# Two layers of outlook attention: softmax, shift matmuls, bands and contractions of layer 1 one to two columns later, with five input buffers and three band buffers

## The chip, the core and the metric

The kernel runs on one core of a Trainium2 chip. A core has five engines with instruction streams of their own: TensorE (matmuls and transposes), VectorE, ScalarE, GpSimd and SyncE, and 16 DMA engines that move data between the device memory and the core's SBUF. TensorE writes to PSUM. The metric is the device time of one execution in microseconds. A profiled execution gives the trace that is read here; in its pages PE is TensorE, PEld the weight loads of TensorE, DVE VectorE, ACT ScalarE, POOL GpSimd and SP SyncE.

## What is computed

The input x has 8 images of 56 x 56 positions and 384 channels, in float32. Two layers are applied one after the other, each with a group normalisation (32 groups) ahead of it and a residual around it:

```python
x = x + layer0(gn(x))    # 12 heads, attention of 9 x 9 logits per position and head, folded back
x = x + layer1(gn(x))    # 6 heads, attention of 9 logits per position and head
```

The change is in layer 1:

```python
a  = x_map @ W_attn + b_attn                            # 9 logits per head and position
a  = softmax(a.reshape(B, H * W, heads, 9), axis=-1)
v  = x_map @ W_v + b_v
vp = pad(v, 1)                                          # patches: the 3 x 3 neighbourhood
y  = einsum('bpKhd,bphK->bphd', patches, a)             # 9 neighbours, weighted
y  = y @ W_proj + b_proj
```

So each position takes logits and values from a projection, a softmax over nine neighbours, a weighted sum over the 3 x 3 neighbourhood of v for each of six heads of 64 channels, and an output projection.

## The kernel before

**Two stages.** Layer 0 runs first and lasts to about 2356 us of the span; layer 1 follows. TensorE's instructions are held in program order (lines 119 and 122). The other engines' instructions are ordered by a scheduler, which may move an instruction ahead of others whose inputs come later.

**Groups and steps of layer 1.** Images are worked on in four pairs, and the 56 columns of a pair in eight groups of PX = 7 columns: 32 groups, of 7 x 112 positions (two images of 56 rows). The loop (line 932) takes one step per column, written as (g, m), group and column in the group. For its main part it is a software pipeline: while the logits and values of group g are made, group g-1 goes through softmax, contraction and output projection.

**The chain of a group.**

- `load` (line 718) brings the group's input, transposed, from memory into a buffer x1t, on SyncE's queue. There are four buffers: three in the pool io1, and one (each fourth group) in the pool late0 of layer 0.
- `normed` (line 728, instructions at line 740) is the group normalisation on ScalarE, from x1t to xn, in two parts of three and four columns.
- `attend` (line 769) takes 128 positions: six matmuls, 2.2 us, to 54 logits and 384 values. VectorE adds the biases (lines 779 and 782), and ScalarE issues stores of v to a table in memory (line 296). Eight columns are seven tiles of 128 positions, so the attend of every eighth column is left out.
- `regroup` (line 789) stores the logits of a group to memory (line 796, ScalarE's queue, written lgtab) and reads them back with the image row across the partitions (line 804, SyncE's queue, written at).
- `weigh` (line 813) is the softmax: maximum and difference on VectorE (818, 819), Exp on ScalarE (820), sum and reciprocal on VectorE (822, 823), and the multiplication on GpSimd (824).
- `move` (line 826): 0/1 matmuls with shifted identities (pw) bring a row's weights to its neighbours; ScalarE copies them into a diagonal layout wz (845), which is stored to a table ztab (847, ScalarE's queue).
- `fetch` (line 855) loads the value patches vp (361) and the bands z (308), both on SyncE's queue, and appends 14 jobs. Four of them are contractions: for each of two images, tiles 0 to 3 in two pairs. Tile b_t makes pc in PSUM by up to 12 small matmuls of z and vp each, and ScalarE copies pc to yT (883). There are two PSUM buffers for pc (NC = 2). Between the contractions lie the last transposes of the group before, and six further jobs are the output projection (po, 899) with the first three transposes (pt, copied at 912, and stored at 914).

**Who sets the order.** Jobs are taken in order of their appending, two per step (`jobs.run`), once due. Before the change the loop calls weigh(g-1) in the step of m = 2, and move(g-1) and fetch(g-1) in that of m = 3, with the jobs due four steps later. So TensorE's order through a group is: pw of the group, then projections of the group before, with attends and transposes between, then the contractions, at the columns m = 0 to 3 of the next group.

**The band buffers.** Layer 0 has two band tiles `zs`; layer 1 uses the halves of these as four band buffers, so that the two images of a group alternate between pairs.

Of the kernel before, what the change touches and what calls it, by code (L numbers as in the profile page):

```python
# [15 lines left out]
def two_outlook_layers(  # L16
# [32 lines left out]
    nc = tc.nc  # L49
# [3 lines left out]
    NCH = C // P  # L53
    IMG = 2
    R = IMG * H
    MARGIN = 2
# [8 lines left out]
    PX = 7  # L65
    NPX = W // PX
    T = IMG * H * PX
# [14 lines left out]
    PY0, NPY0, SX0, SY0 = 7, 8, PX + 4, 11  # L82
    ROW0 = HEADS0 * PX
    WT = 2 * SX0 - E0
    PY1, NPY1, SX1, SY1 = 8, 7, PX + 2, 10
    ROW1 = HEADS1 * PX
# [217 lines left out]
    def bands(queue, z, table, line, slot, row, top, groups, b, py, npy):  # L304

        for (s0, s1), (m0, m1) in groups:
            first = (b * H + top) * line + s0 * slot + m0 * row
            queue.dma_start(
                z[s0:s1, :, m0 * row : m1 * row],
                bass.AP(  # L310
                    table.tensor, table.offset + first + bands.at[row],
                    [[slot, s1 - s0], [py * line, npy], [1, (m1 - m0) * row]],
                ),
            )
# [65 lines left out]
    def layer0(late, pools):  # L380
# [14 lines left out]
        def stats_chunk(pair, blk, i, alone):  # L395

            nm = f"{pair}_{blk}"
            if blk == 0 and i == 0:
                stats[pair] = stat.tile([P, NCH, IMG, NBLK, 6], F32, tag="st0", name=f"st0_{pair}")
            if i == 0:  # L400
                xts[pair, blk] = io.tile([P, NCH, XB, R], F32, tag="xt", name=f"xt_{nm}")
            xr, xt = xrs[pair, blk], xts[pair, blk]
            if alone:
                pt = bank(P, 0, XB * R).rearrange("p (m r) -> p m r", m=XB)
            else:
                pt = ps.tile([P, XB, R], F32, tag="t", name=f"pt_{nm}_{i}")
            for j in range(XB):
                transpose(pt[:, j, :], xr[:, j, i * P : (i + 1) * P], ident[:R, :R])
            nc.scalar.copy(xt[:, i], pt)
            for b in range(IMG):  # L410
                nc.vector.bn_stats(stats[pair][:, i, b, blk, :], xt[:, i, :, b * H : (b + 1) * H])
            if i == NCH - 1:
                nc.sync.dma_start(
                    xTs[pair][:, :, blk * XB * R : (blk + 1) * XB * R], xt.rearrange("p i m r -> p i (m r)")
                )
                del xrs[pair, blk], xts[pair, blk]

        stats_load(0, 0, nc.sync)
# [292 lines left out]
    def layer1(pools, base, last_of_layer0, late_w):  # L711
# [3 lines left out]

        x1ts, lgs = {}, {}

        def load(g):
            pair, px = divmod(g, NPX)

            if g % 4 == 3:
                t = late_w.tile([P, NCH, T], F32, tag="xres", name=f"x1t_{g}")
            else:
                t = io.tile([P, NCH, T], F32, tag="x1t", name=f"x1t_{g}", bufs=3)
            nc.sync.dma_start(t, x1s[pair][px])
            x1ts[g] = t.rearrange("p i (m r) -> p i m r", m=PX)

        def normed(g, m0, m1):
# [28 lines left out]

        NW = SX1 * K * ROW1
        wzs = [fixed.tile([R, NW + PX + 1], F32, name=f"wz1_{n}") for n in range(2)]

        NZ = 4
        half_z = NPY1 * PY1 * ROW1
        zs1 = [
            zs[n // 2].rearrange("p n e -> p (n e)")[: SX1 * SY1, n % 2 * half_z : (n % 2 + 1) * half_z]
            .rearrange("p (n e) -> p n e", n=NPY1)
            for n in range(NZ)
        ]

        def attend(g, m):

# [55 lines left out]
        def move(g):  # L826
# [25 lines left out]
                wz[:, :NW].rearrange("r (s e) -> r s e", s=SX1),  # L852
            )

        def fetch(g, due):
            pair, px = divmod(g, NPX)
            n_tile = 2
            yT = projected(f"1_{g}")
            x1t = x1ts.pop(g)
            vps = [patch_tiles(f"1_{g}", b)[: SX1 * SY1, :NPY1] for b in range(IMG)]  # L860
            for b in range(IMG):
                rows_to_patches(vps[b], vtab1, px, b * H + MARGIN - 1, PY1, NPY1, SX1)
            for b in range(IMG):
                z, vp = zs1[(g * IMG + b) % NZ], vps[b]
                bands(
                    nc.sync, z, ztab1[g % NTAB], LINE1, SLOT1, ROW1, MARGIN - 1, GROUPS1,
                    b, PY1, NPY1,
                )

                def contract(t, b=b, z=z, vp=vp):  # L870
                    lo, hi = t * n_tile, min(NPY1, (t + 1) * n_tile)
                    pc = ps.tile([P, NCH, n_tile, PY1, PX], F32, tag="c", name=f"pc1_{g}_{b}_{t}", bufs=NC)
                    for py in range(lo, hi):
                        zp = z[:, py].rearrange("s (y h m) -> s y h m", y=PY1, h=HEADS1)
                        for h in range(HEADS1):
                            i, j = divmod(h, P // D1)
                            matmul(
                                pc[j * D1 : (j + 1) * D1, i, py - lo],
                                vp[:, py, h * D1 : (h + 1) * D1],
                                zp[:, :, h, :],  # L880
                                start=True, stop=True,
                            )
                    nc.scalar.copy(
                        yT[:, :, :, b, lo * PY1 : hi * PY1],
                        pc[:, :, : hi - lo].rearrange("p i n y m -> p i m (n y)"),
                    )

                for t in range(0, (NPY1 + n_tile - 1) // n_tile, NC):
                    jobs.add(due, lambda t=t, f=contract: [f(t + n) for n in range(NC)])

                    jobs.add(due, turning.pop(0) if turning else lambda: None)

            def project_out(half, j):
                lo, hi = HALVES[half]
                n = (hi - lo) * R
                po = ps.tile([P, 4 * R], F32, tag="of"[(half * NCH + j) % 2], name=f"po1_{g}_{half}_{j}")
                project_half(po, wo_t, yT, half, j)
                res = x1t[:, j, lo:hi].rearrange("p m r -> p (m r)")
                nc.vector.scalar_tensor_tensor(  # L899
                    res, po[:, :n], bo_t[:, j : j + 1], res, ALU.add, ALU.add  # L900
                )

            def turn(m):

                half = m // 4
                lo, hi = HALVES[half]
                if m == lo:
                    fetch.ot = io.tile([R, 4, C], F32, tag="ot", name=f"ot_{g}_{half}")
                pt = banks[-1][:R, :C] if m % 2 else ps.tile([R, C], F32, tag="t", name=f"pt1_{g}_{m}")
                for i in range(NCH):  # L910
                    transpose(pt[:, i * P : (i + 1) * P], x1t[:, i, m, :], ident)
                nc.scalar.copy(fetch.ot[:, m - lo, :], pt)
                if m == hi - 1:
                    nc.sync.dma_start(
                        of[pair * R : (pair + 1) * R, px * PX + lo : px * PX + hi, :],
                        fetch.ot[:, : hi - lo],
                    )

            out, back = project_out, turn
            for work_of in (  # L920
                (lambda: out(0, 0),), (lambda: out(0, 1),), (lambda: out(0, 2),),
                (lambda: out(1, 0), lambda: back(0)), (lambda: out(1, 1), lambda: back(1)),
                (lambda: out(1, 2), lambda: back(2)),
            ):
                jobs.add(due, lambda work_of=work_of: [w() for w in work_of])
            for m in range(3, PX):
                turning.append(lambda m=m: back(m))
# [1 line left out]
        turning = []  # L929
        NG = NPAIR * NPX  # L930
        stage(0)
        for step in range(NG * PX + 4):
            g, m = divmod(step, PX)
            jobs.run(base + step, 1)
            if step == 0:
                last_of_layer0(base + step + 5)
            if step == 4:
                for wz in wzs:
                    nc.gpsimd.memset(wz, 0.0)
            if g < NG:  # L940
                attend(g, m)
            if g and m == 0:
                regroup(g - 1)
                stage(g)
            if m == 4 and g + 1 < NG:
                load(g + 1)
            if m == 6 and g + 1 < NG:
                normed(g + 1, 0, 3)
            if m == 0 and 0 < g < NG:
                normed(g, 3, PX)  # L950
            jobs.run(base + step, 1)

            if g and m == 2:
                weigh(g - 1)
            if g and m == 3:
                move(g - 1)
                while not clear_bands.done:
                    jobs.run(None, 1)
                fetch(g - 1, base + step + 4)
        jobs.run(None, -1)  # L960
        for w in turning:
# [45 lines left out]
```

## Time and profile before

| | |
|---|---|
| time, median of three | 3598.7 us (3592.17 to 3605.03) |
| span of the profiled execution | 3610.8 us, granted TensorE clock 0.978 |
| TensorE busy | 3460.6 us, 96%, 29078 instructions |
| VectorE, ScalarE, GpSimd busy | 1914.9, 1165.1, 986.4 us |
| layer 0 | 0 to about 2356 us |
| layer 1 | about 2356 us to the end, 32 groups; 36.4 to 37.4 us each |
| moved by DMA | 840.73 MB, 233 GB/s on average |

The columns of the views are told where they are shown. In the views of groups and of the timeline, a line such as "L883 ACT COPY yT<-pc" names the line of the kernel, the engine, the operation, and output and input by the program's names. In brackets at the end of a timeline line stands the engine's idle time just before, with what ended it. Instructions that issue a DMA are marked SPq or ACTq; they take a place in the queue of their engine and the transfer itself goes on elsewhere.

The chain that ended last gives TensorE 78% of the span and DMA 16%. The DMA part holds the bands' way to memory and back (5% and 3%), and the logits' (2% and 1%).

### The profile page before, as it was taken

To read this page: it belongs to the slowest core of one execution; us is meant where nothing else is said; L and a number is where in the kernel's file an instruction comes from. 1 tells how busy PE (TensorE), PEld (TensorE's weight loads), DVE (VectorE), ACT (ScalarE), POOL (GpSimd) and SP (SyncE) were. 2 spreads that over 40 slices of the span, in tenths; PEclk is the share of its full clock that TensorE was granted. 3 is DMA by queue.
4 is the path that set the end of the run, shared out by engine and by line. 5 is a ranking of instruction groups with operands and counts; after the bars stand their busy time and mean duration, and the time that the engine had idled before them with its cause. 6 is when DMAs were issued, how large, how long until landed. Compare 5 with 4: busy or idle time off the path is not lost.

```text
span 3610.8 us, 72232 instructions
## 1 busy us (share of the span) xinstructions
PE 3460.6 (96%) x29078; PEld 2375.8 (66%) x29078; DVE 1914.9 (53%) x4648; ACT 1165.1 (32%) x2727; POOL 986.4 (27%) x1409
## 2 busy tenths in 40 slices
PE   4999999999999999999999999989999999999998
PEld 4667767777777777777767777655565565556555
DVE  3766666667666676667666666532222222222222
ACT  2333322332333333333222322232333433333332
POOL 2444334434444434443444444410000000000000
PEclk6999999999999999999999999999999999999999
DMA  9799988688886778887667777677778787777876
GB/s 294 202 285 292 267 265 257 226 249 263 267 271 208 263 238 254 261 258 262 204 208 241 218 223 231 222 252 188 207 200 220 206 226 196 199 218 198 219 196 159
DMA packets 692253, 840.73 MB, mean 233 GB/s; under 512 B 302222, under 2 KB 596174, under 8 KB 687822
## 3 DMA queue, kind: packets, MB, share of 16 engines
q1 hardware_dynamic: 329614, 576.00, 51.1%
q10 hardware_dynamic: 362304, 260.11, 27.5%
q8 instruction: 229, 3.75, 0.5%
q14 instruction: 106, 0.87, 0.1%
HBM read 514.32 MB, written 321.66 MB: 232 GB/s over the span
## 4 chain that ended last, share of the span: by engine, by line
PE 78%; DMA 16%; DVE 2%; ACT 1%; issue 1%; POOL 1%; ACTq 0%; SPq 0%; POOLq 0%; DVEq 0%
PE bank L119 44%; PE po L119 15%; PE pc L119 11%; DMA ztab<-wz 5%; PE pw L119 4%; DMA z<-ztab 3%; DMA lgtab<-lgt 2%; PE pt L122 2%; DMA at<-lgtab 1%; DMA xr<-in_x 1%; PE bank L122 1%; DMA vtab<-v 1%; DMA x1t<-x 1%; DMA xT<-xt 1%; DMA vp<-vtab 1%
## 5 line engine op out<-in xcount | busy, mean ns | idle before, releaser
L119 PE MATMUL bank<-wa_t,xn 128*112 128x288 f32 x4032 | 1083.6, 408 | 2.2 <-ACT xn L471 2.2
L119 PEld LDWEIGHTS bank<-wa_t,xn 128*112 128x112 f32 x4032 | 691.9, 177 | 253.1 <-issue 31.9
L510 POOL TENSOR_TENSOR at<-at,den 112x972 f32<-112x972 f32 x224 | 504.9, 2254 | 1226.6 <-DVE den L509 1181.7
L119 PE MATMUL po<-yT,wo_t 128*128 128x448 f32 (+1 forms) x2304 | 823.7, 497 | 5.4 <-DVE x1t L621 4.8
L119 PEld LDWEIGHTS po<-yT,wo_t 128*128 128x128 f32 x2304 | 435.3, 192 | 296.2 <-issue 192.2
L119 PE MATMUL pc<-z,vp 121*32 121x49 f32 (+1 forms) x17664 | 490.0, 255 | 50.6 <-DMA z<-ztab 23.1
L119 PEld LDWEIGHTS pc<-z,vp 121*32 121x32 f32 (+1 forms) x17664 | 444.2, 131 | 127.5 <-issue 91.8
L119 PE MATMUL bank<-wc_t,xn 128*128 128x438 f32 x1176 | 485.7, 549 | 3.8 <-DMA wc_t<-in_wv 2.6
L486 DVE TENSOR_REDUCE mx<-bank 112x36 f32<-112x324 f32 x672 | 327.1, 487 | 299.5 <-PE bank L119 292.9
L119 PE MATMUL bank<-wv_t,xn 128*128 128x384 f32 x1176 | 418.6, 492 | 0.0
L824 POOL TENSOR_TENSOR at<-at,den 112x378 f32<-112x378 f32 x32 | 30.2, 945 | 1142.4 <-DVE den L823 704.8
L487 DVE TENSOR_TENSOR at<-bank,mx 112x324 f32<-112x324 f32 x672 | 328.5, 489 | 21.1 <-DVE mx L486 0.5
L491 ACT ACTIVATE at<-at 112x972 f32<-112x972 f32 x224 | 227.1, 1014 | 331.7 <-DVE at L487 307.9
L119 PEld LDWEIGHTS bank<-wc_t,xn 128*128 128x128 f32 x1176 | 216.3, 193 | 177.9 <-issue 167.2
L740 ACT ACTIVATE xn<-x1t,bias,scale 128x168 f32<-128x168 f32 (+4 forms) x498 | 213.6, 503 | 322.1 <-DMA x1t<-x 227.9
L119 PEld LDWEIGHTS bank<-wv_t,xn 128*128 128x128 f32 x1176 | 219.5, 191 | 139.5 <-issue 18.6
L899 DVE SCALAR_TENSOR_TENSOR x1t<-po,bo_t,x1t 128x448 f32<-128x448 f32 (+1 forms) x192 | 120.1, 626 | 339.6 <-PE po L119 339.6
L555 ACT COPY wt<-pw 112x120 f32<-112x120 f32 x224 | 58.0, 259 | 662.1 <-PE pw L119 577.5
L533 POOL TENSOR_TENSOR pre<-at,at 112x108 f32<-112x108 f32 (+1 forms) x440 | 238.0, 541 | 115.0 <-DVE wt L556 100.6
L779 DVE TENSOR_TENSOR lgt<-bank,ba_t 128x54 f32<-128x54 f32 x196 | 41.1, 210 | 417.2 <-PE bank L119 417.1
L503 DVE TENSOR_TENSOR d<-at 112x432 f32<-112x432 f32 x224 | 141.1, 630 | 196.9 <-ACT at L491 196.9
L600 ACT COPY yT<-pc 128x294 f32<-128x294 f32 x256 | 103.3, 408 | 372.1 <-PE pc L119 318.8
(81 smaller groups left out, 2845.4 us busy)
## 6 DMA issues: line engine op xcount, KB each, us to landing
z<-ztab SPq DMA_DIRECT2D x64, 2352.0 KB
vp<-vtab SPq DMA_DIRECT2D x64, 1536.0 KB
ztab<-wt ACTq DMA_DIRECT2D x336, 183.8 KB
vp<-vtab SPq DMA_DIRECT2D x64, 945.0 KB
xT<-xt SPq DMA_DIRECT2D x56, 672.0 KB
xin<-xT ACTq DMA_DIRECT2D x56, 672.0 KB
xres<-xT SPq DMA_DIRECT2D x32, 1176.0 KB
x1t<-x SPq DMA_DIRECT2D x32, 1176.0 KB
```

Source lines behind the costliest of these rows:

```text
L119: tc.keep_in_program_order(nc.tensor.matmul(*args, **kwargs))
L122: tc.keep_in_program_order(nc.tensor.transpose(*args, **kwargs))
L486: nc.vector.tensor_reduce(mx[:, pi, :], pl.rearrange("r q a -> r a q"), AX.X, ALU.max)
L487: nc.vector.tensor_tensor(at[:, pi], pl, mx[:, pi, :].unsqueeze(1).to_broadcast([R, K2, PH]), ALU.subtract)
L491: nc.scalar.activation(at, at, AF.Exp, scale=SCALE0)
L503: nc.vector.tensor_add(d4, at[:, :, 0:4], at[:, :, 4:8])
L510: nc.gpsimd.tensor_tensor(at, at, den.unsqueeze(2).to_broadcast([R, K, K2, PH]), ALU.mult)
L533: nc.gpsimd.tensor_tensor(dst, terms[0], terms[1], ALU.add)
L555: nc.scalar.copy(mid[:, 0 : E0 : E0 - 1, :], pw[:, 0 : E0 : E0 - 1, :])
L600: nc.scalar.copy(yT[:, :, :, b, rows_of], pc.rearrange("p i n y m -> p i m (n y)"))
L740: nc.scalar.activation(to[:, i, :, rows], x1ts[g][:, i, lo - first : hi - first, rows], AF.Identity, bias=bias[:, i, b : b + 1], scale=sca ...
L899: nc.vector.scalar_tensor_tensor(res, po[:, :n], bo_t[:, j : j + 1], res, ALU.add, ALU.add)
```

## The change

Softmax, shift matmuls, bands and contractions of a group are each placed later in the loop, so that the waits between them have more time. The input load goes one column earlier. As a group then stays open for longer, a fifth input buffer is taken, out of the fourth half of the band tiles, and the band buffers go from four to three. The band loads get a function of their own, called right behind the shift matmuls, and the loop runs two steps longer. The store of a transposed input in the opening part of layer 0 is held in program order.

| step of a group in the loop | before | after |
|---|---|---|
| load of the next input | m = 4 | m = 3 |
| weigh | m = 2 | m = 3 |
| move | m = 3 | m = 4 |
| band loads | m = 3, behind vp | m = 4 |
| vp loads, jobs appended | m = 3 | m = 5 |
| contractions run at the next group's | m = 0 to 3 | m = 2 to 5 |

```diff
@@ stats_chunk (layer 0)
-                nc.sync.dma_start(
+                store = nc.sync.dma_start(
                     xTs[pair][:, :, blk * XB * R : (blk + 1) * XB * R], xt.rearrange("p i m r -> p i (m r)")
                 )
+                if alone:
+                    tc.keep_in_program_order(store)
@@ layer1
+        NZ = 3
+        half = NPY0 * PY0 * ROW0 // 2
+        halves = [z.rearrange("p n e -> p (n e)")[:, n * half : (n + 1) * half] for z in zs for n in range(2)]
...
-            if g % 4 == 3:
+            if g % 5 == 3:
                 t = late_w.tile([P, NCH, T], F32, tag="xres", name=f"x1t_{g}")
+            elif g % 5 == 4:
+                t = halves[3][:, : NCH * T].rearrange("p (i t) -> p i t", i=NCH)
             else:
                 t = io.tile([P, NCH, T], F32, tag="x1t", name=f"x1t_{g}", bufs=3)
...
-        NZ = 4
-        half_z = NPY1 * PY1 * ROW1
-        zs1 = [
...
+        zs1 = [t[: SX1 * SY1, : NPY1 * PY1 * ROW1].rearrange("p (n e) -> p n e", n=NPY1) for t in halves[:NZ]]
...
+        def fetch_bands(g):
+            for b in range(IMG):
+                bands(
+                    nc.sync, zs1[(g * IMG + b) % NZ], ztab1[g % NTAB], LINE1, SLOT1, ROW1, MARGIN - 1,
+                    GROUPS1, b, PY1, NPY1,
+                )
...
-        for step in range(NG * PX + 4):
+        for step in range(NG * PX + 6):
...
-            if m == 4 and g + 1 < NG:
+            if m == 3 and g + 1 < NG:
                 load(g + 1)
...
-            if g and m == 2:
+            if g and m == 3:
                 weigh(g - 1)
-            if g and m == 3:
+            if g and m == 4:
                 move(g - 1)
                 while not clear_bands.done:
                     jobs.run(None, 1)
+                fetch_bands(g - 1)
+            if g and m == 5:
                 fetch(g - 1, base + step + 4)
```

More of the change, by code (lines that the diff above doesn't have):

```diff
@@ L716, in layer1 @@
         x1ts, lgs = {}, {}
+        NZ = 3
+        half = NPY0 * PY0 * ROW0 // 2
+        halves = [z.rearrange("p n e -> p (n e)")[:, n * half : (n + 1) * half] for z in zs for n in range(2)]
+        assert half >= NPY1 * PY1 * ROW1 and half >= NCH * T
         def load(g):
             pair, px = divmod(g, NPX)
-            if g % 4 == 3:
+            if g % 5 == 3:
                 t = late_w.tile([P, NCH, T], F32, tag="xres", name=f"x1t_{g}")
+            elif g % 5 == 4:
+                t = halves[3][:, : NCH * T].rearrange("p (i t) -> p i t", i=NCH)
             else:
@@ L759, in layer1 @@
         wzs = [fixed.tile([R, NW + PX + 1], F32, name=f"wz1_{n}") for n in range(2)]
-        NZ = 4
-        half_z = NPY1 * PY1 * ROW1
-        zs1 = [
[L764 to L767, printed above, removed]
+        zs1 = [t[: SX1 * SY1, : NPY1 * PY1 * ROW1].rearrange("p (n e) -> p n e", n=NPY1) for t in halves[:NZ]]
         def attend(g, m):
@@ L864, in fetch @@
                 z, vp = zs1[(g * IMG + b) % NZ], vps[b]
[L865 to L868, printed above, removed]
                 def contract(t, b=b, z=z, vp=vp):
```

## The prediction

> **What bounds the kernel now.** I read the page's shares first: TensorE is busy 3460.6 of 3610.8 us (96%). Then a table of windows, to see in which layer the other 4% lie. Its columns are the window, its length, busy time and count of TensorE, its weight loads, VectorE, ScalarE and GpSimd, the granted clock, the DMA share and GB/s.
>
> ```profile
> 1000.00:1100.00 100.00, 100.00 (x1103) 72.38 (x1102) 68.00 (x172) 34.22 (x70) 40.20 (x56) 1.00 0.77 234
> 2800.00:2900.00 100.00, 95.06 (x772) 59.55 (x771) 28.36 (x62) 39.76 (x123) 2.84 (x3) 1.00 0.80 208
> 3000.00:3100.00 100.00, 93.82 (x600) 57.30 (x601) 26.07 (x56) 35.45 (x109) 2.23 (x3) 0.95 0.82 212
> ```
>
> Layer 0 (up to about 2356) leaves TensorE no gap; layer 1 leaves 4 to 6 us in 100. Layer 1 is 1255 us with 1173.5 busy: 81.5 us idle. So the change can win at most about 82 us and the clock loss that goes with it; other engines have room. The waits of TensorE in 2500 to 3550 (28 groups of seven columns, 54 of 1050 us idle) name the causes (total, times, longest):
>
> ```profile
> PE pw L119 <- POOL at L824: 19.1, 13, 3.7
> PE pc L119 <- DMA z<-ztab: 18.6, 11, 3.1
> PE pc L119 <- issue: 10.3, 5, 3.3
> PE pc L119 <- ACT yT L883: 4.3, 7, 0.8
> ```
>
> The 0/1 matmuls pw wait for the softmax's last multiplication, the contractions pc for their bands z. Both are the same chain, logits to memory and back, softmax, pw, bands to memory and back, contractions, reaching TensorE a little late. That is what the change loosens.
>
> A short gap costs twice:
>
> ```profile
> 3439.65 2.82 PE L119 MATMUL pc<-z,vp 90*64 90x56 f32 x48 [3.29 <-issue]
> ```
>
> 48 contraction matmuls after 3.29 us of idling take 2.82 us; elsewhere 1.61.
>
> [...] gaps of 2.2 us are already followed by slow stretches. [...] at 2906.55 ScalarE issues stores that stand behind five normalisations which run only from 2906.91:
>
> ```profile
> 2906.48 0.53 ACT L740 ACTIVATE xn<-x1t,bias,scale 128x168 f32<-128x168 f32 x1 [11.21 <-DMA x1t<-x]
> 2906.55 0.78 ACTq L296 DMA_DIRECT2D vtab<-v  x2
> 2906.91 2.18 ACT L740 ACTIVATE xn<-x1t,bias,scale 128x168 f32<-128x168 f32 x5
> ```
>
> [...]
>
> ```profile
> 2652.91 1.78 SPq L308 DMA_DIRECT2D z<-ztab  x4
> 2655.11 0.38 ACTq L796 DMA_DIRECT2D lgtab<-lgt  x1
> 2662.70 0.31 SPq L804 DMA_DIRECT2D at<-lgtab  x1
> 2665.36 0.83 DVE L818 TENSOR_REDUCE mx<-at 112x42 f32<-112x378 f32 x1 [8.24 <-DMA at<-lgtab]
> ```
>
> The logit store goes out 2.2 us behind the band loads and its read can be issued only 7.6 us later; the maximum starts 12.4 us after the z issue. At 2944.28 and 3246.93 it is the same (12.9 and 12.5). Where the store is alone, issue to maximum is about 7 us.
>
> **The change part by part.** No instruction is added or removed, and TensorE's order in layer 0 is unchanged. What moves is seen in the instruction orders of the two built kernels.
>
> Layer-0 store kept in order: the orders of layer 0 stay as they were, cost 0.
>
> TensorE: pw goes from ahead of the projections to between the contraction tiles 1_1 and 1_2. Its 6 matmuls (0.75 us) are the same. GpSimd is done about 6.8 us after the maximum (0.83+0.55+0.52+0.84+0.42, the multiplication 0.95, and hand-overs), which is t=29.6 with the walk below, and pw now stands at t=35: the wait of 19.1 goes.
>
> Bands: they now have from the ztab store behind that pw to the first contraction of the next group. I set t=0 at the start of the last transposes of a group. The store goes at -2.0. From ztab store to z issue is 9.1 to 14.1, mostly 12.3 to 13.2; I take 12.8, so z is issued at 10.8 and lands at 17 to 18. The first contraction stands at 20 (17.8 where no attend precedes it): the wait of 18.6 nearly goes as well.
>
> Five inputs: the scheduler uses the extra buffer to move the load of the next input, and its normalisation on ScalarE, nearly a whole group forward. In SyncE's order the x1t load now stands right behind the vp loads and ahead of z, and waits for the transposes that free its buffer. It goes out at about t=0. From issue to the first normalisation the trace shows 8.4 to 8.7 us (2861.03 to 2869.5, 2897.75 to 2906.48), 14.6 with vp ahead of it. ScalarE stands at it until t=9 to 11, then runs 11 to 15 normalisations of 0.42 to 0.57. The x1t wait was 217.6 us on ScalarE in this window before, so this alone is not new.
>
> **The step that decides** is what stands behind them. After the normalisations ScalarE has the logit store, transposed copies, the yT copy of contraction tile 0_0, then **Exp**, and only then the yT copy of 0_1. Before, Exp stood behind the yT copies of 0_0, 0_1 and of tiles 1_0 and 1_1. The contractions have two PSUM buffers, so tile 0_3 can't start before yT 0_1 is copied: TensorE now waits there for the softmax. Two VectorE additions of an attend stand behind the maximum in the same way.
>
> When is Exp done? The logit store goes when the attend of m=0 has its sums, t=12, just behind z at 10.8. So each group has the collision shown above, and the maximum runs at 10.8+12 = 22.8 (22 to 24). To yT 0_1: maximum 0.93, logits 0.13, v 0.55 (the subtraction beside it), stores 0.8, a copy 0.38, yT 0_0 0.33, Exp 0.42, yT 0_1 0.45: 4.0, with hand-overs 4.2. Tile 0_3 can start at t=27.
>
> When does TensorE reach it? From starts in the trace: transposes 0.4, three projections of 448 at 2.25, three of 336 at 1.7, three attends at 2.2, three more sets of transposes, two contraction pairs at 1.54, tile 0_2 and one more attend: t=25.0, and 22.8 for half of the groups, where the attend ahead of it is the skipped one (column 0 mod 8). The stall is 2.0 or 4.2; as a stall moves the next group too I take 2.8. Such gaps drop the clock; 48 matmuls lost 1.2 us above, part of the gaps do it, plus the projection behind them: 1.6. A group is then 34.6 (its TensorE work) +2.8+1.6 = 39.0. Before: 34.6+1.9 idle (54/28) +0.9 clock = 37.4.
>
> Sum: +1.6 x 27 groups = +43. The last groups, with no input left to load, lose their waits: -5. The tail, where pw and pc waited 2.66 and 2.37, gets -6 with the clock. Start of layer 1 (16 us idle to 2500, on weights and first inputs) I leave at 0, with 8 either way: three inputs are loaded up front, and one waits for the clearing of its half of the bands, which ended near 2392. 3598.7+43-5-6 = 3630.
>
> **The rivals.** A: the waits vanish and nothing replaces them. For it: pw, z and x1t all get room, and 1.5 us off the chain (a logit store not behind z) brings the stall to about 0.5. Against: the collision is seen three times where the trace has this spacing. Work: 1.9+0.9 per group gone is 28 x 2.8 = 78, less what remains of start and end: 3525; with a stall of 0.5 up to 3560. Chance 0.32. B: the new wait is as long as the old ones, 1.5 us less than I take: 3585 to 3600. Chance 0.11. C, my forecast's kind: the stall is 2 to 4 us per group: 3610 to 3685, likeliest 3630. Chance 0.57; part of it is the case that x1t lands as late as 14.6 us behind its issue, so that the logit store leaves ScalarE 1.5 us later: 3650 to 3685.
>
> **How the numbers follow.** Cases C give slower 0.57, B 0.11 is the middle (within 0.3% is 3588 to 3609.5), A 0.32 faster. The range must take in most of A's part: 3545 leaves out its lower half, about 0.13, and 3685 leaves out 0.05.
>
> **What would show it.** In the changed kernel the pw wait and the z wait of TensorE should be gone in 2500 to 3550, and a wait of pc for a yT copy (ScalarE L883's counterpart) of 2 to 4 us should stand in nearly each group, with Exp right ahead of that copy. The maximum should start about 12 us behind the z issue. The spacing of z issues should be 39 against 36.4 to 37.4, and the clock lower. If the logit read comes back within 10 us of the z issue, or x1t normalises by t=8, the stall is not there and A is right.

## The result and the profile after

The changed kernel takes 3636.85 us (median of 4, 3635.32 to 3641.92), against 3595.43 us for the kernel before on the same chip. The ratio is 1.0115, with a 95% interval of 1.0089 to 1.0141: about 41 us slower.

The loss is in layer 1: from 2356 us on, the profiled execution takes 1284.0 us, that of the kernel before 1254.8, and the first projection of layer 1 starts no later (2352.9 against 2356.2 us). The waits of TensorE in 2500 to 3550 are the first view to read (line waited for, total, times, longest). The kernel after has only these two there:

```profile
PE pc L119 <- ACT yT L888: 69.9, 41, 4.5
PE po L119 <- ACT yT L888: 2.9, 4, 0.8
```

The waits of pw for GpSimd (19.1 us) and of the contractions for their bands (18.6 us) are gone, as the change intends. In their place the contractions wait for a copy of a contraction tile out of PSUM (line 888, line 883 before): 69.9 us in place of 4.3. Idle time in this window went from 54.1 to 72.9 us (1050 less the busy time below), and the clock from 0.98 to 0.96:

```profile
2500.00:3550.00 1050.00, 977.15 (x7256) 609.57 (x7256) 276.98 (x604) 371.89 (x1103) 25.50 (x27) 0.96 0.77 202
2700.00:2800.00 100.00, 87.42 (x676) 55.29 (x676) 24.75 (x54) 31.15 (x92) 2.83 (x3) 0.90 0.70 179
```

The columns are those of the windows in the prediction. The second line is one of the worst stretches: 12.6 us idle and a mean clock of 0.90. On the chain that ended last the bands' way to memory and back is down from 5% and 3% to 2% and 2%, and the logits' is up from 2% and 1% to 5% and 3%.

One group of the trace shows the chain that ends in the stall. The lines are put in order of time from the timelines of ScalarE, SyncE, VectorE and TensorE; each has start, duration, and in brackets the idle time just before.

```profile
2759.38 0.34 SPq L734 DMA_DIRECT2D x1t<-x  x1
2768.75 1.78 SPq L308 DMA_DIRECT2D z<-ztab  x4
2770.17 0.53 ACT L749 ACTIVATE xn<-x1t,bias,scale 128x168 f32<-128x168 f32 x1 [8.99 <-DMA x1t<-x]
2771.80 1.52 ACTq L798 DMA_DIRECT2D lgtab<-lgt  x1
2780.80 0.31 SPq L806 DMA_DIRECT2D at<-lgtab  x1
2783.36 0.83 DVE L820 TENSOR_REDUCE mx<-at 112x42 f32<-112x378 f32 x1 [8.50 <-DMA at<-lgtab]
2784.22 0.55 DVE L784 TENSOR_TENSOR v<-bank,bv_t 128x384 f32<-128x384 f32 x1
2784.81 0.79 ACTq L296 DMA_DIRECT2D vtab<-v  x2
2785.63 0.48 ACT L917 COPY ot<-pt 112x384 f32<-112x384 f32 x1 [7.25 <-DVE at L821]
2786.01 0.44 ACT L888 COPY yT<-pc 128x336 f32<-128x336 f32 x1
2786.34 0.53 ACT L822 ACTIVATE at<-at 112x378 f32<-112x378 f32 x1
2786.51 1.60 PE L119 MATMUL pc<-z,vp 90*64 90x56 f32 x36 [3.42 <-ACT yT L888]
2786.76 0.44 ACT L888 COPY yT<-pc 128x336 f32<-128x336 f32 x1
2786.91 0.84 DVE L824 TENSOR_REDUCE den<-at 112x42 f32<-112x378 f32 x1 [1.19 <-ACT at L822]
2788.18 0.55 DVE L784 TENSOR_TENSOR v<-bank,bv_t 128x384 f32<-128x384 f32 x1
2788.76 1.86 ACTq L296 DMA_DIRECT2D vtab<-v  x2
2790.66 0.64 ACT L888 COPY yT<-pc 128x336 f32<-128x336 f32 x2 [3.08 <-issue]
2791.16 2.81 PE L119 MATMUL pc<-z,vp 90*64 90x56 f32 x48 [2.23 <-ACT yT L888]
```

The bands go out at 2768.75 and the logits 3.05 us behind them. The read of the logits can be issued only 9 us after their store, and the maximum starts at 2783.36, after VectorE has stood still for 8.5 us. Behind it, in VectorE's queue, is the addition for v of an attend that TensorE did long before; behind that addition, in ScalarE's queue, are the stores of v, a transposed copy, the copy of 0_0, Exp and the copy of 0_1. ScalarE stood still for 7.25 us. TensorE lost 3.42 us at its contractions, waiting for work that needs nothing of the softmax.

The tile that waited is 0_2 (the 36 matmuls are those of 0_2 and 0_3). It starts at 2786.51, when the copy of 0_0 is done (2786.01 + 0.44), and Exp stands behind that copy. A second wait follows. The sum of the softmax waits on VectorE for Exp, and behind it stands the addition for v of the next attend. The stores of this v, whose issue ends only at 2790.62, stand ahead of the copy of 0_2 in ScalarE's queue, and tile 1_0, which takes the same PSUM buffer, loses another 2.23 us. Over all of 2500 to 3550, 46.1 us of the wait end with the copy of 0_0 (20 waits), 11.3 us with that of 0_1 (6) and 12.6 us with that of 0_2 (15).

### The profile page after: what moved, and what is told of

It reads as the page before. It is cut to its first block, busy times and chain, and to the rows that moved or that the text cites. A ratio compares the mean times of both kernels' runs of the same rounds, so it can differ in the third digit from the quotient of the medians.

```text
span 3640.0 us, 72231 instructions
## 1 busy us (share of the span) xinstructions
PE 3475.3 (95%) x29078; PEld 2387.3 (66%) x29078; DVE 1911.7 (53%) x4648; ACT 1169.5 (32%) x2727; POOL 986.3 (27%) x1409
## 4 chain that ended last, share of the span: by engine, by line
PE 76%; DMA 16%; DVE 3%; ACT 2%; ACTq 1%; issue 1%; POOL 1%; SPq 0%; DVEq 0%; POOLq 0%
PE bank L119 43%; PE po L119 14%; PE pc L119 11%; DMA lgtab<-lgt 5%; PE pw L119 4%; DMA at<-lgtab 3%; DMA x1t<-x 2%; PE pt L122 2%; DMA ztab<-wz 2%; DMA z<-ztab 2%; ACTq L296 1%; DMA xr<-in_x 1%; PE bank L122 1%; DMA z<-x 1%; DVE v L784 1%
## 5 line engine op out<-in xcount | busy, mean ns | idle before, releaser
L119 PE MATMUL pc<-z,vp 121*32 121x49 f32 (+1 forms) x17664 | 498.3, 256 | 87.5 <-ACT yT L888 73.6
L119 PE MATMUL bank<-wc_t,xn 128*128 128x438 f32 x1176 | 501.5, 564 | 3.6 <-DMA wc_t<-in_wv 2.5
L749 ACT ACTIVATE xn<-x1t,bias,scale 128x168 f32<-128x168 f32 (+4 forms) x402 | 169.1, 502 | 204.3 <-DMA x1t<-x 186.2
L904 DVE SCALAR_TENSOR_TENSOR x1t<-po,bo_t,x1t 128x448 f32<-128x448 f32 (+1 forms) x156 | 97.4, 624 | 228.0 <-PE po L119 228.0
```

Of the source, the lines that this page charges most:

```text
L119: tc.keep_in_program_order(nc.tensor.matmul(*args, **kwargs))
L749: nc.scalar.activation(to[:, i, :, rows], x1ts[g][:, i, lo - first : hi - first, rows], AF.Identity, bias=bias[:, i, b : b + 1], scale=sca ...
L904: nc.vector.scalar_tensor_tensor(res, po[:, :n], bo_t[:, j : j + 1], res, ALU.add, ALU.add)
```

## The experiments

The theory: the scheduler puts the maximum and Exp of the softmax ahead of other work on VectorE and ScalarE, so that late logits stop that work, and TensorE with it. The rivals: the five inputs, with their early normalisation, make the logits late and cost the time by themselves; the bands hold the logits up wherever the softmax stands. The kernel before took 3608.9 us on the chip of the first four experiments and 3588.3 us on that of the last three, so the ratios are what is to be compared.

### Exp alone in program order

```diff
-            nc.scalar.activation(at, at, AF.Exp)
+            tc.keep_in_program_order(nc.scalar.activation(at, at, AF.Exp))
```

> Exp alone is held in program order, so on ScalarE it comes behind the yT copies of contraction tiles 0_0 to 0_3; the maximum keeps its place on VectorE, ahead of the additions of an attend. If Exp is what holds TensorE at tile 0_3, its wait for yT (69.9 us in 2500 to 3550) falls below 15 us and the time to 3540-3570. If the maximum is (the v additions behind it, the v stores on ScalarE that wait for these, and the yT copies behind the stores), only Exp's 0.4 us per group is won: the wait stays at 50-60 us and the time at 3615-3630. I take the second. If it is neither but the late bands or inputs, nothing changes: 3637.

Measured: 3612.66 us, ratio 1.0014 (1.0003 to 1.0026). TensorE's waits in the same window:

```profile
PE pc L119 <- ACT yT L888: 40.4, 21, 5.5
PE pw L119 <- POOL at L826: 6.1, 4, 1.5
```

Exp is behind the copies, and 40.4 of 69.9 us of wait remain. No wait is left for the copy of 0_1, and 35.2 of the 40.4 us are for that of 0_0, which stands behind the stores of v. So Exp is a part of the block, and what stands behind the maximum is the larger part. (The maximum was not pinned alone.) The Exp part was more than I gave it: instead of 50 to 60 us, 40.4 were left, and the time came out about 10 us below my interval (1.0014 x 3598.7 = 3604).

### Maximum and Exp in program order, softmax at m = 3

```diff
-            nc.vector.tensor_reduce(mx, at.rearrange("r x k h -> r x h k"), AX.X, ALU.max)
+            tc.keep_in_program_order(
+                nc.vector.tensor_reduce(mx, at.rearrange("r x k h -> r x h k"), AX.X, ALU.max)
+            )
...
-            nc.scalar.activation(at, at, AF.Exp)
+            tc.keep_in_program_order(nc.scalar.activation(at, at, AF.Exp))
```

> The maximum and Exp are both held in program order, with the softmax called at m = 3 as in the changed kernel: behind the additions of three attends. My theory: the wait for yT goes (below 5 us), but the maximum can't run before t=29, GpSimd is done at 36, and pw stands at 33, so a wait of pw for GpSimd of about 3 us per group takes its place: 3600-3640. If the order on VectorE and ScalarE isn't the cause, the wait for yT stays near 70 us.

Measured: 3572.85 us, ratio 0.9904 (0.9878 to 0.9929). The waits:

```profile
PE pw L119 <- POOL at L828: 26.7, 26, 2.9
PE pt L122 <- ACT ot L919: 0.2, 1, 0.2
```

The wait for yT is gone altogether, and pw waits for GpSimd in nearly every group. The kind was as expected; the size was not: about 1 us per group, not 3. From the maximum to the multiplication's end it takes about 4.5 us here (0.83+0.55+0.52+0.84+0.42+0.95 and hand-overs), where I had worked with 6.8. In the kernel before it was 5.0 at the median.

### The same, with the softmax at m = 2

```diff
-            if g and m == 3:
+            if g and m == 2:
                 weigh(g - 1)
```

together with the two edits of the experiment before.

> The maximum and Exp are both held in program order, and the softmax is called at m = 2: the maximum stands behind the additions of two attends, Exp behind the yT copies of 0_0 and 0_1. My theory: the maximum can run at t=24.5, later than the logits come (22 to 24), nothing that TensorE needs stands behind it, GpSimd is done at 31 and pw stands at 33: no wait is left in most groups, and the time is 3530-3560. If the logits' late arrival costs time wherever the softmax stands, or the inputs do, it stays above 3600.

Measured: 3535.1 us (3531.87 to 3540.81), ratio 0.9799 (0.9772 to 0.9825). This version beats both kernels. What is left of TensorE's waits, and VectorE at a maximum (timeline):

```profile
PE pc L119 <- ACT yT L890: 7.1, 6, 2.5
PE po L119 <- ACT yT L890: 3.0, 4, 0.8
PE pt L122 <- ACT ot L919: 1.2, 3, 0.8
```

```profile
2753.07 0.55 DVE L784 TENSOR_TENSOR v<-bank,bv_t 128x384 f32<-128x384 f32 x1
2753.76 0.84 DVE L821 TENSOR_REDUCE mx<-at 112x42 f32<-112x378 f32 x1
```

The maximum has no bracket: the logits were there, and it follows the addition for v directly. So it is in 21 of the 29 groups of this window; in the other 8 the maximum waits for the logits, 17.3 us in all (166.9 us, in all 27 groups, in the changed kernel). The logits come no sooner than in the changed kernel: their read is issued 8.4 us behind their store at the median, against 7.9. So late logits cost next to nothing here, where nothing urgent is queued behind them. The spacing of the maxima is 34.8 us in the mean, close to the 34.6 us of TensorE's work per group.

Whether moving the softmax to m = 2 without the pinning would do anything is not shown: no run has the one without the other.

### Four inputs instead of five

```diff
-            if g % 5 == 3:
+            if g % 4 == 3:
                 t = late_w.tile([P, NCH, T], F32, tag="xres", name=f"x1t_{g}")
-            elif g % 5 == 4:
-                t = halves[3][:, : NCH * T].rearrange("p (i t) -> p i t", i=NCH)
```

> The five input buffers are undone (four again), the rest is as changed. My theory: the orders on ScalarE, VectorE and TensorE stay nearly the same, the load of an input still goes out behind the last transposes, and the stall at contraction tile 0_3 stays: 3625-3650, wait for yT 60-80 us. The rival, that the fifth buffer's early load and normalisation are what makes the logits late: the wait for yT falls below 25 us and the time to 3560-3605.

Measured: 3683.54 us, ratio 1.0205 (1.0171 to 1.0239). Slower still, which neither theory had:

```profile
PE bank L119 <- ACT xn L747: 51.3, 26, 4.2
PE pc L119 <- ACT yT L886: 39.0, 21, 3.8
```

The projections now wait for the normalised input. I had seen that the load keeps its place behind the last transposes, but not that with four buffers the buffer freed there takes the input of the very next group, where with five it takes that of the group after. The fifth buffer is not the cause of the loss; it prevents a larger one.

### Half of the bands

From the fourth group on, the band loads of the second image are left out; its contractions run on bands that lie there from earlier groups.

```diff
-            for b in range(IMG):
+            for b in range(IMG if g < 3 else 1):
```

> The changed kernel with the band loads of the second image left out from the fourth group on (its contractions run on old bands); all else stays. If the band loads hold up the logits' way through memory, half of them gone brings the maximum from 12.5 us behind the z issue to about 10, the store of the logits to the maximum from 11.1 to about 9, the wait of pc for yT from 69.9 to 20-35 us and the time to 3575-3605. If the logits are late because ScalarE stands behind the normalisations, nothing changes (3630-3640).

Measured: 3579.04 us, ratio 0.9972 (0.9960 to 0.9984).

```profile
PE pc L119 <- ACT yT L888: 29.6, 32, 3.0
PE po L119 <- ACT yT L888: 3.1, 4, 0.9
```

Over the groups of the window, the maximum comes 10.8 us behind the first z issue at the median instead of 13.2 (the expectation has 12.5), and 8.8 us behind the logit store instead of 11.1. The wait for yT falls from 69.9 to 29.6 us. So the bands do hold up the logits, by 2.3 us for half of them. The run moves fewer bytes at other times too; but the kernel before, with all its bands, agrees. In the three groups of the window where it issues the bands 2.2 to 3.5 us ahead of the logit store, the maximum comes 8.9 to 10.3 us behind the store; in the others it is 6.0 to 8.5. Lateness and queue order together make the stall: half of the bands away takes more than half of the wait away, the other order nearly all of it.

### Five inputs alone, on the kernel before

The input and band buffers of the change in the kernel before; all columns as before.

```diff
+        NZ = 3
+        half = NPY0 * PY0 * ROW0 // 2
+        halves = [z.rearrange("p n e -> p (n e)")[:, n * half : (n + 1) * half] for z in zs for n in range(2)]
...
-            if g % 4 == 3:
+            if g % 5 == 3:
                 t = late_w.tile([P, NCH, T], F32, tag="xres", name=f"x1t_{g}")
+            elif g % 5 == 4:
+                t = halves[3][:, : NCH * T].rearrange("p (i t) -> p i t", i=NCH)
...
```

> The kernel before with only the five input buffers and three band buffers of the change; columns as before. My theory: inputs didn't hold TensorE before (no wait of a projection for a normalisation), so the time stays within 0.5% of before. If the fifth buffer alone brings the normalisations in front of the logit store and makes the logits late, it is slower by 20 us or more, with more wait of pw for GpSimd than before's 19.1 us.

Measured: 3590.83 us, ratio 1.0006 (0.9988 to 1.0024): no difference. The wait of pw for GpSimd is 13.0 us here (19.1 before), that of the contractions for their bands 20.1 (18.6). The buffers alone neither help nor harm; they matter once a group stays open longer, as the next experiment shows.

### Pinned softmax at m = 2 with four inputs

The edits of the pinned kernel at m = 2 and of the one with four inputs, together.

> The softmax pinned and called at m = 2, but four input buffers instead of five. With four the projections waited 51.3 us for normalisations. If that wait comes from groups that stay open two columns longer and so free an input later, it stays at 40-60 us and the time is 3580-3610. If ScalarE was only held up by the softmax ahead of the normalisations, it goes, and the time is 3535-3550.

Measured: 3600.27 us, ratio 1.0028 (1.0015 to 1.0042).

```profile
PE bank L119 <- ACT xn L747: 48.9, 29, 4.2
PE pc L119 <- ACT yT L888: 3.6, 3, 1.4
```

The wait for normalisations stays at 48.9 us with the softmax out of the way. So it comes from the buffers and not from ScalarE standing at the softmax. The four kernels with moved columns make a table:

| ratio to before | four inputs | five inputs |
|---|---|---|
| softmax placed by the scheduler | 1.0205 | 1.0115 (the change) |
| softmax pinned at m = 2 | 1.0028 | 0.9799 |

## Why the prediction was right, point by point

- **The old waits vanish.** Forecast: the pw wait and the z wait go. Both are absent from the waits of 2500 to 3550.
- **The logits.** With t=0 at a group's last transposes, medians over 27 groups of the trace: x1t issue 0.5, first normalisation 10.1, z issue 9.9 (forecast 10.8), logit store 12.0 (forecast 12), maximum 23.1 (forecast 22.8). The maximum stands 13.2 us behind the first z issue (forecast 12).
- **The stall.** Forecast 2.8 us per group. Measured 72.9 us of idle time in 1050/38.8 = 27.1 groups: 2.7. That the two are so close is in part luck. The walk has one wait, at tile 0_3 for the copy of 0_1, 4.2 us behind the start of the maximum. Measured, the main wait is at tile 0_2, which TensorE reaches about 0.8 us sooner, for the copy of 0_0, which is done about 3.1 us behind the start of the maximum; both ends are early by about as much. And 0.5 us of the 2.7 are the second wait, for the copy of 0_2, which the walk hasn't got. (The walk also names two contraction pairs ahead of tile 0_3, with which its items come to about 26. The trace has one there, and with it t=25.0 is right: tile 0_2 is reached at 24.2 in the group shown.)
- **A group.** Forecast 39.0 us. From one maximum to the one 24 groups later it is 38.8 us each, against 37.4 to 37.6 in the kernel before (single groups from 33 to 41 us there). What is left for the clock is 38.8-34.6-2.7 = 1.5 (forecast 1.6, an estimate that starts from the 1.2 us lost behind one gap), a remainder that rests on the 34.6 of the forecast. The trace shows the kind of this loss. Behind the gap of 3.42 us that ends at 2786.51 the granted clock is still 1.00 up to 2787.0, 0.85 in the next 0.5 us, and 0.50 from 2787.5 to 2797.5. The gap of 2.23 us lies in this stretch; the 48 matmuls behind it take 2.81 us instead of 1.61, and the six matmuls of the attend that follows take 4.29 instead of 2.47. Two more stretches at 0.50, at gaps of 2.61 us (up to 2703.96) and 4.31 us (up to 2743.55), make up the rest of the loss in the 0.90 of 2700 to 2800. In the kernel before, the clock is 0.50 from 3438.5 to 3445.0, from within the gap of 3.29 us on, and from 2619.5 to 2622.5 behind a gap of 2.21 us, where 48 matmuls take 2.37 us.
- **The sum.** Forecast +31 on 3598.7, measured +41 between the two medians, but 29.2 between the two profiled executions: that of the kernel before took 3612.7 us, 17 above its median of 3595.4. In these two, +25.3 lie between the first and the last maximum, where I had 43-5 = +38, +1.1 ahead of the first maximum, where I had 0, and +2.8 behind the last, where I had -6. In the tail one stall of 1.9 us stands in place of the pw and pc waits of 3.7 and 2.4, so these waits did shrink as forecast, and the time didn't. How the 41 us split can't be told from one profile of each kernel.
- **What was not exact.** I named Exp as the deciding step and the maximum as acting "in the same way". The wait that I had named, for the copy of 0_1 behind Exp, is 11.3 of 69.9 us; 46.1 us are for the copy of 0_0, which stands ahead of Exp in most groups and behind the stores of v, and so behind the maximum. The first experiment agrees: with Exp moved away 40.4 us stayed. In four of the 27 groups the copy of 0_1 even stands ahead of Exp in ScalarE's order, and TensorE still waits. And the way from maximum to the end of the multiplication, given as 6.8 us, takes about 5.8 in the changed kernel (23.1 to 28.0, and 0.95), 5.0 in the kernel before and 4.5 where nothing stands between; this changed nothing in the forecast, because pw stood behind the stall, but it made the expectation for m = 3 too slow.
- **The rival A**, 3525 to 3560, is not what the change does. It is what its later shift matmuls, bands and contractions reach once two instructions are pinned and the softmax is called at m = 2: ratio 0.9799, 3526 on 3598.7. The change was held back by an order that it doesn't write down.

What stays open: why the logit read is issued 9 us after a store that is itself one instruction. The half bands show that the bands cause a part; the runs do not separate what remains into the other transfers under way and the trip through memory itself. The maximum alone was not pinned, so its share and that of Exp are read from the trace and from one experiment.

## What to carry to other kernels

When a step's input comes through memory, look at what stands behind the first instruction that waits for it, on each engine. Here the wait cost what was queued there, not what the step costs: the contractions' wait for yT in 2500 to 3550 was 69.9 us with urgent work behind the maximum and Exp, and 7.1 us with the two pinned at m = 2. Where a scheduler orders an engine, the place of a call in the program is not the place of its instructions in the engine's order: with the softmax called at m = 3, Exp ran behind the copy of 0_3 when it was pinned, and in most groups between those of 0_0 and 0_1 when it was not. Holding one or two instructions in program order can be what makes a move take place. A pipeline that is opened longer needs its input buffers counted again: the fifth buffer was worth nothing before the move and about 2.3% after it with the pinned softmax (0.9799 against 1.0028).

## What was not expected of the hardware

The logits' way to memory and back was longer where the bands were issued just ahead of it: from logit store to maximum 6.9 us at the median in the kernel before, where the bands go out about 10 us ahead, 11.1 with all bands about 2 us ahead, 8.8 with half of them. So leaving out half of the bands' bytes gave back about 2.3 of 4.2 us. In what way the bands hold up the logits is not shown.
